# A fused attention-MLP-SSM kernel: the MLP's product a x GELU(g) moved from VectorE to ScalarE and GpSimd

## Chip, core and metric

One core of a Trainium2 chip, float32 throughout. The metric is the device time of one execution in microseconds; the time before is the median of three runs. The engines are TensorE (PE; its weight loads are shown apart as PEld), VectorE (DVE), ScalarE (ACT), GpSimd (POOL) and SyncE (SP), which here only starts DMAs.

## What is computed

x has 4096 tokens of 256. It is layer-normalized, two independent branches read the normalized tokens, and the output is x plus both. One branch is a Mamba block, the other a local transformer of two layers. Cut to what matters here, each transformer layer is:

```python
h = shift_token(x)                        # half of the channels come from the token before
q, k, v = split(h @ wqkv)                 # 8 heads of 64
q, k = rotary_xpos(l2norm(q) * qs, l2norm(k) * ks)
x = x + local_attention(q, k, v) @ wo     # windows of 128, each looks at itself and the one before
h = layernorm(shift_token(x)) * lg + lb   # over the 256 channels
a, g = split(h @ w1 + b1)                 # 682 columns each
x = x + (a * gelu(g)) @ w2 + b2           # gelu by erf
```

The Mamba block projects x to 512 channels and a gate, convolves over 4 tokens, and runs for each channel and each of 16 states the recurrence h = exp(dt*A)*h + dt*x*B over all tokens, sums h*C over the states, gates and projects back.

## The kernel before

**Tiling.** The transformer works in stages of 256 tokens: 2 layers x 16 stages = 32, each with two attention windows of 128. The Mamba block works in 8 blocks of 512 tokens, 4 groups of 128 channels, 16 states; two states are handled together, so `recur` runs 8 times for each block and channel group. In it GpSimd multiplies dt*x by the spread B (L793), ScalarE makes the decays exp(dt*A) in PSUM (L802), VectorE scans along the tokens (L807) and multiplies by the spread C (L817), ScalarE keeps the last column (L813), for some pairs GpSimd adds the two states (L825), and TensorE transposes and sums them into a PSUM bank y (L829). `bc` names the spread tiles, of which there are six.

**Projection and rotary (L905 to L995).** For each window TensorE makes q, k and v (L918, into PSUM banks `mm`). ScalarE squares and VectorE sums for the norms (L929, L931, L972). VectorE multiplies q by the two rotary tables (L963, L965), GpSimd adds the two products (L945). k is scaled by VectorE (L978), multiplied twice by GpSimd (L985), added by it (L945). TensorE transposes both (L950), ScalarE copies them out (L956). The products live in the buffer `turn`: five tiles, taken by two for q, one for the scaled k and two for its products. A work on q's matmuls holds its two tiles before it starts.

**Attention** scores, masks (L1032, a maximum goes to `top`), exponentiates (L1042), transposes (L1057), mixes (L1075) and projects out (L1116).

**The MLP stage (`mlp`, from L1134).** GpSimd adds the two halves of the channels (L1153), TensorE takes the mean, and so the layer norm proceeds to `hn` (L1171). The 682 columns of g and a are cut into five chunks of 128 and a last of 42. `up` (L1180) makes two chunks a time in one of five PSUM banks. `gates` does g: ScalarE evicts each chunk with its bias into `u` (L1196), the buffer `mlp` of one tile of 6 x 256 columns. The last chunk of g shares a matmul with the last chunk of a; ScalarE evicts that piece of a into `a5` (L1208). One ScalarE instruction takes GELU of all of `u` (L1217), between two loads of activation tables. GpSimd multiplies the last 42 rows by `a5` (L1222). `gated` then does the five other chunks of a: its matmuls wait for `u` after GELU, and VectorE adds the bias and multiplies by GELU(g) in one instruction for each chunk, from PSUM into `u` (L1230). `down` (L1243 in layer 0, L1262 in layer 1) multiplies by w2.

**Order.** The order isn't that of the program text. Each step is recorded by `add` with its engine, an estimated cost, what it reads and writes, and a lead `soon`. A step's key is its due time (`plan.key`, in stages; one stage of the transformer is 1.0) less `soon`. `Plan.order` simulates the engines with the estimated costs and buffers that come free, and gives each engine, when it is free, the ready step of the lowest key among those not over AHEAD beyond the earliest open one. So the leads and AHEAD fix each engine's queue; at run time the queues are in order and synchronized by semaphores. Buffers (L350 to L386) give tiles in the order of recording, the banks to whoever comes first. `port=True` marks VectorE steps that the planner keeps apart from GpSimd's.

The steps that the prediction speaks of also include: normalization of x (L579 to L606), the sum of x and attention, `mid` (L1122), the second in-projection products (L762 to L770), the finish (L546), and the Mamba output (L846 to L879).

Of the kernel before, what the change touches and what calls it, by code (L numbers as in the profile page):

```python
# [27 lines left out]
P = 128  # L28
# [14 lines left out]
AHEAD = 2.400000  # L43
# [275 lines left out]
def mamba_and_local_transformer(  # L319
# [27 lines left out]
    def buffer(name, n, shape, pool=work, any_first=False):  # L347
# [12 lines left out]
    turns = buffer("turn", 5, [P, HEADS, 2, DH // 2])  # L360
# [9 lines left out]
    lasts = buffer("a5", 1, [LAST, TS])  # L370
    small = {n: buffer(n, k, [P, w]) for n, k, w in (
        ("mv", 2, 2 * NW), ("rstd", 2, NW), ("nrm", 4, 2 * HEADS), ("top", 2, HEADS), ("den", 2, HEADS), ("mcol", 3, 1), ("tail", 2, CI * (TAPS - 1)),
# [82 lines left out]
    def load_small():  # L455
        dma(96, lambda: xpw.ap, lambda: xp_wT.rearrange("(c p) n -> p c n", p=P), writes=[xpw], soon=-0.27)
        for at_row in (0, DH):
            dma(32, lambda at_row=at_row: dtw.ap[at_row : at_row + DTR], lambda: dt_wT, writes=[(dtw, at_row)], soon=0.09)
        dma(128, lambda: b2row.ap, lambda: b2_d[DEPTH - 1 : DEPTH, :].partition_broadcast(P), writes=[b2row], soon=0.34)

    def load_qkv(l):
        for s in range(3):
            cut = slice(s * INNER, (s + 1) * INNER)
            dma(
                512, lambda cut=cut: wqkv.ap[:, :, cut],
                lambda cut=cut: wqkv_d[l][:, cut].rearrange("(k p) n -> p k n", p=P), writes=[(wqkv, s)], soon=-0.12,
            )

    def load_rest(l):
        dma(512, lambda: wo.ap, lambda: wo_d[l].rearrange("(h p) n -> p h n", p=P), writes=[wo], soon=-0.18)  # L470
        for half in range(2):
            for m, n in ((0, WHOLE), (NM - 1, LAST)):
                to, of = w1_at(half, m), half * HID + m * MC
                dma(
                    n, lambda to=to, n=n: w1.ap[:, :, to : to + n],
                    lambda of=of, n=n: w1_d[l][:, of : of + n].rearrange("(k p) n -> p k n", p=P),
                    writes=[(w1, (half, m))], soon=-1.18,
                )
# [3 lines left out]
            lambda: w2_d[l][0:whole, :].rearrange("(m p) n -> p m n", p=MC), writes=[(w2, 0)], soon=-1.27,  # L482
        )
        dma(42, lambda: w2.ap[0 : HID - whole, NM - 1, :], lambda: w2_d[l][whole:HID, :], writes=[(w2, 1)], soon=0.27)
# [28 lines left out]
        add("PE", 8.3, shift, [w1], [pb], soon=-0.56)  # L513
        add("DVE", 0.4, bias, [pb], [b1, b1x], soon=-1.5)
        add("DVE", 4.6, scale, [], [w1], port=True, soon=-0.19)
# [14 lines left out]
    def base_of(s):  # L530

        base = plan.value(rows_b)
        if s in sums:
            dma(256, lambda: base.ap, lambda: sums[s].ap, [sums[s]], [base], soon=-1.01)
            return base
        dma(256, lambda: base.ap, lambda: rows(x, s), writes=[base], soon=-0.2)
# [3 lines left out]
            ), [b2row], [base], soon=-1.46,  # L540
# [3 lines left out]
    def finish(s, po, base):  # L544

        add("DVE", 0.6, lambda: nc.vector.tensor_tensor(base.ap, halves(po), base.ap, ALU.add), [po], [base], soon=-1.31)  # L546
        if s in sums:
            dma(256, lambda: rows(out, s), lambda: base.ap, [base], soon=0.15)
            return
        sums[s] = plan.fixed(dram.tile([P, NW, D], F32, tag=f"sum{s}", name=f"sum{s}"))  # L550
        dma(256, lambda: sums[s].ap, lambda: base.ap, [base], [sums[s]], soon=0.04)
# [4 lines left out]
    def shift_column(l, s):  # L556
        now = xts[l, s]
        if s == 0:
            add("POOL", 0.14, lambda: nc.gpsimd.memset(now.ap[:, 1, 0:1], 0.0), [], [(now, 0)], soon=-0.23)
        else:  # L560
# [3 lines left out]
                [(old, 1)], [(now, 0)], soon=-0.63,  # L564
            )

    def normalize(s):
# [5 lines left out]
        dma(256, lambda: xb.ap, lambda: rows(x, s), writes=[xb], soon=0.01)  # L573
# [27 lines left out]
        add("DVE", 1.1, stats, [xb], [mv], soon=1.38)  # L601
        add("ACT", 0.5, root, [mv], [rstd], soon=0.58)
        add("DVE", 0.6, centre, [mv, rstd], [xb], port=True, soon=0.31)
        now = xts[0, s] = plan.value(tokens)
        add("PE", 0.44, turn, [xb], [pt], holds=[now], soon=0.21)
        add("ACT", 0.48, lambda: nc.scalar.copy(now.ap[:, :, 1:], halves(pt)), [pt], [(now, 1)], soon=0.22)  # L606
        shift_column(0, s)
        dma(256, lambda: xn_d[s].ap, lambda: now.ap[:, :, 1:], [(now, 1)], [xn_d[s]], soon=0.0)
# [3 lines left out]
    def reload(s):  # L612
        now = xts[1, s] = plan.value(tokens)
        dma(256, lambda: now.ap[:, :, 1:], lambda: x1_d[s].ap, [x1_d[s]], [(now, 1)], soon=-1.33)
# [6 lines left out]
    def in_half(i):  # L621
# [3 lines left out]
            lambda: in_wT[:, i * DI : (i + 1) * DI].rearrange("(k p) n -> p k n", p=P), writes=[w], soon=-0.73,  # L625
# [3 lines left out]
    def in_proj(b, w, c, to):  # L629
# [9 lines left out]
        add("PE", 1.72, emit, [w, xms[b]], [pm], holds=[to], soon=-0.05)  # L639
        return pm  # L640

    def front_load(b):
        xm = xms[b] = plan.value(xms_b)
        for i in range(PB):
            s = b * PB + i
            dma(
                256, lambda i=i: xm.ap[:, :, i * TS : (i + 1) * TS], lambda s=s: xn_d[s].ap, [xn_d[s]], [(xm, i)], soon=0.1
# [5 lines left out]
    def front_conv(b, c, w):  # L653
        xin, xc, tail = plan.value(rows_m), xcs[b], tails[b]
        edge = slice(c * (TAPS - 1), (c + 1) * (TAPS - 1))
        if b == 0:
            add("POOL", 0.14, lambda: nc.gpsimd.memset(xin.ap[:, 0 : TAPS - 1], 0.0), [], [(xin, 0)], soon=0.0)
        else:
# [3 lines left out]
                [(old, c)], [(xin, 0)], soon=-0.7,  # L662
            )
        pm = in_proj(b, w, c, xin)
        add("ACT", 0.48, lambda: nc.scalar.copy(xin.ap[:, TAPS - 1 :], pm.ap), [pm], [(xin, 1)], soon=0.34)
        if b < NB - 1:
            add(
                "POOL", 0.14, lambda: nc.gpsimd.tensor_copy(tail.ap[:, edge], xin.ap[:, TB:]), [(xin, 1)], [(tail, c)], soon=-0.09
            )
# [13 lines left out]
        for j in range(TAPS - 1):  # L683
            add("DVE", 0.7, lambda j=j: tap(j), [xin, pm], [(xc, c) if j == TAPS - 2 else pm], soon=1.05)

    def silu(v):
# [4 lines left out]
        add("ACT", 4.52, emit, [], [v], soon=0.03)  # L691

    def front_dbl(b):
# [3 lines left out]
        def emit():  # L697
# [9 lines left out]
        add("PE", 1.75, emit, [xc, xpw], [px], holds=[xd, part], soon=-0.05, part="columns")  # L707
        add("ACT", 0.48, lambda: nc.scalar.copy(part.ap[0:n, 0:TB], px.ap[DH : DH + n]), [px], [part], alone=[px], soon=-0.78)
        add(
            "DVE", 0.6, lambda: nc.vector.tensor_tensor(xd.ap[0:n], px.ap[0:n], part.ap[0:n, 0:TB], ALU.add),  # L710
            [px, part], [(xd, 0)], alone=[px], soon=0.43,
        )

        add("ACT", 0.48, lambda: nc.scalar.copy(xd.ap[DH : DH + DTR], xd.ap[0:DTR]), [(xd, 0)], [(xd, 1)], soon=-0.03)
        xds[b] = xd
        bc = bcs[b] = plan.fixed(dram.tile([2 * NS, TB], F32, tag=f"bc{b}", name=f"bc{b}"))
        dma(64, lambda: bc.ap, lambda: xd.ap[DTR:n, :], [(xd, 0)], [bc], soon=-1.47)

    def gate_conv(b, c, w):
# [4 lines left out]
        add("ACT", 0.48, lambda: nc.scalar.copy(sz.ap[:, c, :], pz.ap), [pz], [(sz, c)], soon=-1.3)  # L724

    def times(b, c):
# [12 lines left out]
        add("PE", 1.15, emit, [xd, dtw], banks2, holds=dts2, soon=0.34, part="rows")  # L739
        for i in range(2):  # L740
# [3 lines left out]
                ), [banks2[i]], [dts2[i]], soon=0.13,  # L744
# [3 lines left out]
    def prepare(b, c):  # L748

        if c % 2 == 0:  # L750
# [7 lines left out]
        add("ACT", 0.6, lambda: nc.scalar.activation(e.ap[:, n], dt.ap, AF.Abs), [dt], [e], soon=-0.9)  # L758
        add("ACT", 0.6, lambda: nc.scalar.activation(dt.ap, dt.ap, AF.Relu), [], [dt], soon=-1.46)
        add("ACT", 0.54, lambda: nc.scalar.activation(e.ap[:, n], e.ap[:, n], AF.Exp, scale=-1.0), [], [e], soon=0.57)  # L760
        add(
            "DVE", 0.36, lambda: nc.vector.tensor_scalar(r.ap[:, n], e.ap[:, n], 1.0, -1.0, ALU.add, ALU.add),  # L762
            [e], [r], port=True, soon=0.51,
        )
        add("POOL", 1.22, lambda: nc.gpsimd.tensor_tensor(r.ap[:, n], e.ap[:, n], r.ap[:, n], ALU.subtract), [e], [r], soon=-1.13)
        add("ACT", 0.6, lambda: nc.scalar.activation(e.ap[:, n], e.ap[:, n], AF.Ln, bias=one_t), [], [e], soon=0.18)
        add("POOL", 1.22, lambda: nc.gpsimd.tensor_tensor(dt.ap, dt.ap, r.ap[:, n], ALU.add), [r], [dt], soon=0.93)
        add("POOL", 1.22, lambda: nc.gpsimd.tensor_tensor(dt.ap, dt.ap, e.ap[:, n], ALU.add), [e], [dt], soon=-0.63)
        add(
            "DVE", 0.61, lambda: nc.vector.tensor_tensor(dtx.ap, dt.ap, xc.ap[:, c, :], ALU.mult),  # L770
            [dt, (xc, c)], [dtx], port=True, soon=-0.25,
# [3 lines left out]
    def recur(b, c, g):  # L775
# [6 lines left out]
        for s in range(2):  # L782
# [4 lines left out]
                .rearrange("n t -> (n t)").partition_broadcast(P), [bc], [w], soon=0.12,  # L787
# [7 lines left out]
            ), [dtx], [u], soon=-0.33,  # L795
        )
        for i in range(NG):
# [6 lines left out]
                ), [dt], [h], soon=0.69,  # L804
# [4 lines left out]
                ), [(u, i), (state, (c, n))], [h], soon=-1.12,  # L809
            )  # L810
            if b < NB - 1:
                add(
                    "ACT", 0.1, lambda h=h, n=n: nc.scalar.copy(state.ap[:, c, n : n + 1], h.ap[:, TB - 1 : TB]),  # L813
                    [h], [(state, (c, n))], alone=[h], soon=-0.07,
# [4 lines left out]
                ), [h, spread[1]], [(u, i)], alone=[h], soon=-0.23,  # L819
# [19 lines left out]
        for i in range(n_sums):  # L839
            add("PE", 0.44, lambda i=i: collect(i), [(u, i)], [y], soon=0.1)  # L840

    def close(b, c):
# [3 lines left out]
        add("ACT", 0.48, lambda: nc.scalar.copy(ytv(), y.ap), [y], [yt], soon=-0.11)  # L846

        def turn():
# [3 lines left out]
        add("PE", 0.44, turn, [yt], [py], soon=-0.54)  # L852
# [3 lines left out]
            ), [py], [(xc, c)], soon=-1.46,  # L856
# [3 lines left out]
            [sz], [(xc, c)], soon=-1.5,  # L860
        )

    def out_load():
# [3 lines left out]
            writes=[w], soon=-0.24,  # L867
# [3 lines left out]
    def out_proj(b, i, w):  # L871
# [12 lines left out]
        add("PE", 3.44, emit, [w, xc, base], [po], soon=-1.0)  # L884
# [5 lines left out]
    def rotation(l, s):  # L890
# [3 lines left out]
            writes=[rot], soon=-0.77,  # L894
        )
        for i, scales in enumerate((qks, qkw)):
            for q in range(2):
# [6 lines left out]
                    ), [rot], [(trig, (i, q))], soon=-0.27,  # L904
# [3 lines left out]
    def project(l, s, t):  # L908
# [19 lines left out]
        def norm(q, pm, sq):  # L928
            add("ACT", 0.48, lambda: nc.scalar.activation(sq.ap, pm.ap, AF.Square), [pm], [sq], alone=[pm], soon=0.5)  # L929
# [3 lines left out]
                ), [sq], [(nrm, q)], soon=-0.97,  # L933
# [10 lines left out]
        def turned(parts, to):  # L944
            add("POOL", 1.22, lambda: nc.gpsimd.tensor_tensor(parts[0].ap, parts[0].ap, parts[1].ap, ALU.add), [parts[1]], [parts[0]], soon=-0.57)  # L945
# [472 lines left out]
```

## Time and profile before

| what | value |
|---|---|
| runs | 1913.62, 1914.05, 1916.52 us; median 1914.05 |
| the profiled execution | 1914.12 us |
| its span, first to last instruction | 1912.3 us |
| mean granted TensorE clock | 0.992 of full |
| instructions | 37355 |
| DMA | 334.79 MB, mean 175 GB/s |

In the profile's groups, "out<-in" names tiles without buffer numbers, then partitions x elements and a count; after the bar stand busy us (overlap counted once), mean ns of one, and the engine's idle just before with what ended it. L numbers are lines of the kernel before. A row of waits is "engine output line <- who released it: us in total, times, longest". Matmul ends are modelled, so a busy TensorE isn't TensorE at its peak; a float32 matmul shows as two instructions.

### The profile page before, as it was taken

How to read it: one execution, taken by the hardware profiler on the slowest of the kernel's cores; microseconds unless marked ns; L12 is line 12 of the kernel's file. 1: busy time of each engine (PE TensorE's matmuls, PEld its weight loads, DVE VectorE, ACT ScalarE, POOL GpSimd, SP SyncE). 2: the span in 40 equal slices, each digit the busy share in tenths (PEclk: the TensorE clock that was granted, in tenths of full speed). 3: DMA queues.
4: the chain of work that ended last, by engine and by line, in shares of the span. 5: the costliest groups of instructions: out<-in, count | busy, mean ns of one | idle time of the engine just before them, and what ended most of it. 6: DMA issues, size and time to landing. Idle time of an engine off the chain costs nothing. (4 is left out here: it accounts for less than half of the span.)

```text
span 1912.3 us, 37355 instructions
## 1 busy us (share of the span) xinstructions
PE 1830.8 (96%) x13184; PEld 1359.3 (71%) x13184; DVE 1725.4 (90%) x3190; ACT 1543.8 (81%) x3634; POOL 1482.8 (78%) x1242
## 2 busy tenths in 40 slices
PE   7999999999999999999989999999999999999986
PEld 3676677776677767776767777777777777777775
DVE  5889899899999999898998799899999899899995
ACT  5887878879877788887977878797888798878673
POOL 3686787788877788877887678987888877887884
PEclk9999999999999999999999999999999999999999
DMA  5553555554555445565564555456455554544653
GB/s 171 177 169 131 171 169 166 183 177 150 174 188 197 157 137 183 173 205 183 190 210 167 180 196 174 161 201 206 133 175 182 183 185 166 183 171 164 200 177 140
DMA packets 133962, 334.79 MB, mean 175 GB/s; under 512 B 13468, under 2 KB 57200, under 8 KB 133776
## 3 DMA queue, kind: packets, MB, share of 16 engines
q1 hardware_dynamic: 133488, 332.21, 52.0%
q8 instruction: 104, 1.70, 0.4%
q14 instruction: 82, 0.67, 0.1%
q10 hardware_dynamic: 288, 0.20, 0.0%
HBM read 315.06 MB, written 17.30 MB: 174 GB/s over the span
## 5 line engine op out<-in xcount | busy, mean ns | idle before, releaser
L793 POOL TENSOR_TENSOR bc<-dtx,bc 128x1024 f32<-128x1024 f32 x256 | 606.0, 2368 | 190.9 <-DMA bc<-bc 146.0
L807 DVE TENSOR_TENSOR_SCAN da<-da,state,bc 128x512 f32<-128x512 f32 x448 | 564.6, 1279 | 52.3 <-ACT da L802 23.3
L802 ACT ACTIVATE da<-dt,negA 128x512 f32<-128x512 f32 x512 | 349.6, 694 | 81.1 <-DVE bc L817 76.4
L918 PE MATMUL mm<-wqkv,xt 128*128 128x512 f32 x768 | 362.2, 603 | 3.5 <-DVE turn L965 1.4
L817 DVE TENSOR_TENSOR bc<-da,bc 128x512 f32<-128x512 f32 x512 | 339.8, 678 | 7.7 <-ACT state L813 5.0
L1180 PE MATMUL mm<-hn,w 128*128 128x256 f32 (+1 forms) x1408 | 333.9, 384 | 7.7 <-DVE top L1032 4.2
L1180 PEld LDWEIGHTS mm<-hn,w 128*128 128x128 f32 (+1 forms) x1408 | 258.0, 189 | 67.2 <-issue 13.9
L825 POOL TENSOR_TENSOR bc<-bc 128x512 f32<-128x512 f32 x192 | 244.4, 1277 | 69.9 <-DVE bc L817 65.6
L1042 ACT ACTIVATE pr<-pr,top 128x256 f32<-128x256 f32 (+1 forms) x512 | 253.3, 500 | 18.2 <-DVE top L1032 17.9
L918 PEld LDWEIGHTS mm<-wqkv,xt 128*128 128x128 f32 x768 | 136.9, 192 | 129.4 <-issue 114.5
L1032 DVE CUSTOM_DVE_ANT_0 pr<-mm,maskf,nrm 128x256 f32<-128x256 f32 (+1 forms) x512 | 212.8, 472 | 6.3 <-PE mm L1017 3.3
L985 POOL TENSOR_TENSOR turn<-turn,trig 128x512 f32<-128x512 f32 x128 | 161.8, 1285 | 57.7 <-DVE turn L978 57.5
L829 PE MATMUL y<-ident,bc 128*128 128x128 f32 x1280 | 180.4, 277 | 19.8 <-POOL bc L825 19.6
L829 PEld LDWEIGHTS y<-ident,bc 128*128 128x128 f32 x1280 | 144.9, 141 | 54.7 <-POOL bc L825 27.6
L945 POOL TENSOR_TENSOR turn<-turn,turn 128x512 f32<-128x512 f32 x128 | 164.0, 1283 | 11.3 <-DVE turn L965 6.9
L1017 PEld LDWEIGHTS mm<-kT,qT 64*128 64x128 f32 x2016 | 125.7, 189 | 36.0 <-issue 12.4
L1017 PE MATMUL mm<-kT,qT 64*128 64x128 f32 x2016 | 145.1, 284 | 5.6 <-ACT kT L956 2.3
L1064 ACT COPY prT<-mm 128x512 f32<-128x512 f32 (+1 forms) x256 | 134.1, 581 | 13.4 <-PE mm L1057 12.5
L813 ACT COPY state<-da 128x1 f32<-128x1 f32 x448 | 70.9, 165 | 87.4 <-DVE da L807 71.5
L1075 PE MATMUL mm<-prT,v 128*64 128x128 f32 x2016 | 140.2, 281 | 0.5
L1075 PEld LDWEIGHTS mm<-prT,v 128*64 128x64 f32 x2016 | 113.9, 137 | 27.2 <-issue 8.0
L635 PE MATMUL mm<-xm,mw 128*128 128x512 f32 x256 | 123.2, 608 | 2.0 <-DVE xc L678 1.3
(132 smaller groups left out, 3370.5 us busy)
## 6 DMA issues: line engine op xcount, KB each, us to landing
bc<-bc SPq DMA_DIRECT2D x512, 512.0 KB, 4.6
io<-in_x SPq DMA_DIRECT2D x32, 256.0 KB, 4.9
mw<-in_in_wT SPq DMA_DIRECT2D x16, 512.0 KB, 5.3
rot<-in_rot SPq DMA_DIRECT2D x32, 128.0 KB, 2.2
xn<-xt SPq DMA_DIRECT2D x16, 256.0 KB, 2.8
xm<-xn SPq DMA_DIRECT2D x16, 256.0 KB, 4.3
x<-mid SPq DMA_DIRECT2D x16, 256.0 KB, 2.8
mw<-in_out_wT SPq DMA_DIRECT2D x8, 512.0 KB, 4.6
```

What stands on the lines that cost most here:

```text
L793: "POOL", 2.35, lambda: nc.gpsimd.tensor_tensor(u.ap, dtx.ap.unsqueeze(1).to_broadcast([P, NG, TB]), u.ap, ALU.mult), [dtx], [u], soon=-0.33,
L802: "ACT", 0.63, lambda h=h, n=n: nc.scalar.activation(h.ap, dt.ap, AF.Exp, scale=negA[:, c * NS + n : c * NS + n + 1]), [dt], [h], soon=0.69,
L807: "DVE", 1.18, lambda h=h, n=n, i=i: nc.vector.tensor_tensor_scan(h.ap, h.ap, u.ap[:, i, :], state.ap[:, c, n : n + 1] if b else 0.0, ALU. ...
L817: "DVE", 0.61, lambda h=h, i=i: nc.vector.tensor_tensor(u.ap[:, i, :], h.ap, spread[1].ap[:, i, :], ALU.mult), [h, spread[1]], [(u, i)], a ...
L825: add("POOL", 1.22, lambda: nc.gpsimd.tensor_tensor(u.ap[:, 0, :], u.ap[:, 0, :], u.ap[:, 1, :], ALU.add), [], [u], soon=-1.5)
L829: nc.tensor.matmul(y.ap[:, t, :], lhsT=u.ap[:, i, t * P : (t + 1) * P], rhs=ident, is_transpose=True, start=g == 0 and i == 0 and t == 0, ...
L918: nc.tensor.matmul(pm.ap, lhsT=hT[k], rhs=wqkv.ap[:, k, q * INNER : (q + 1) * INNER], start=k == 0, stop=k == KC - 1,)
L1017: nc.tensor.matmul(halves(scs[j])[:, i, a * WIN : (a + 1) * WIN], lhsT=qT.ap[half, 2 * g + i, :], rhs=kk.ap[half, 2 * g + i, :], start=n == 0,
L1032: nc.vector.tensor_tensor_reduce(out=prs[j].ap[:, i, keys], in0=halves(scs[j])[:, i, keys], in1=mask[:, keys], scale=nrm.ap[:, h : h + 1], ...
L1042: nc.scalar.activation(prs[j].ap[:, i, keys], prs[j].ap[:, i, keys], AF.Exp, bias=top.ap[:, h : h + 1], scale=-1.0, accum_out=den.ap[:, h ...
L1075: nc.tensor.matmul(hpair(po.ap)[j * DH : (j + 1) * DH, hp, :], lhsT=vv.ap[:, h * DH : (h + 1) * DH], rhs=prT.ap[:, i, j, a, :], start=a == ...
L1180: nc.tensor.matmul(halves(pm)[0:r, i, :], lhsT=w1.ap[:, k, c0 : c0 + r], rhs=hn.ap[:, k, :], start=k == 0, stop=k == KC - 1,)
```

## The change

In the MLP, ScalarE evicts each chunk of a with its bias into a new buffer `ga` of two tiles of 2 x 256 columns, and GpSimd multiplies `u` by it: chunks 0 and 1 in one instruction, 2 and 3 in one, chunk 4 alone, and the last 42 rows as before. The matmuls of a no longer wait for `u`. The tile `a5` becomes the second half of one `ga` tile; chunk 4 takes its first half. `turn` goes from five tiles to four, and the small buffer `nrm` from four to three. AHEAD goes from 2.4 to 2.84, and nearly all of the leads `soon` in the kernel have new values. Instructions elsewhere, and their shapes, are the same.

```diff
-AHEAD = 2.400000
+AHEAD = 2.84
...
-    turns = buffer("turn", 5, [P, HEADS, 2, DH // 2])
+    turns = buffer("turn", 4, [P, HEADS, 2, DH // 2])
...
-    lasts = buffer("a5", 1, [LAST, TS])
+    gains = buffer("ga", 2, [P, 2, TS])
...
-        ("mv", 2, 2 * NW), ("rstd", 2, NW), ("nrm", 4, 2 * HEADS), ("top", 2, HEADS), ("den", 2, HEADS), ("mcol", 3, 1), ("tail", 2, CI * (TAPS - 1)),
+        ("mv", 2, 2 * NW), ("rstd", 2, NW), ("nrm", 3, 2 * HEADS), ("top", 2, HEADS), ("den", 2, HEADS), ("mcol", 3, 1), ("tail", 2, CI * (TAPS - 1)),
...
-        def up(tiles, after=()):
+        def up(tiles):
...
-            add("PE", 0.86 * len(tiles), emit, [hn, w1, *after], [pm], soon=0.11)
+            add("PE", 0.86 * len(tiles), emit, [hn, w1], [pm], soon=0.21)
...
-        add("ACT", 4.1, gelu, [], [u], soon=-1.05)
-        add(
-            "POOL", 0.68, lambda: nc.gpsimd.tensor_tensor(u.ap[0:LAST, last, :], u.ap[0:LAST, last, :], a5.ap, ALU.mult),
-            [a5], [(u, last)], soon=-0.03,
-        )
-
-        def gated(ms):
-            pm = up([(w1_at(0, m), MC) for m in ms], [u])
+        add("ACT", 4.1, gelu, [], [u], soon=-1.42)
+
+        def times_gain(a, m, n, rows=P):
+            at = m % 2
+            add(
+                "POOL", 0.68 if n == 1 else 1.22, lambda: nc.gpsimd.tensor_tensor(
+                    u.ap[0:rows, m : m + n, :], u.ap[0:rows, m : m + n, :], a.ap[0:rows, at : at + n, :], ALU.mult
+                ), [(a, m) if n == 1 else a], [(u, m + i) for i in range(n)], soon=-0.83,
+            )
+
+        times_gain(a45, last, 1, LAST)
+
+        def gated(ms, a):
+
+            pm = up([(w1_at(0, m), MC) for m in ms])
             for i, m in enumerate(ms):
                 add(
-                    "DVE", 0.39, lambda i=i, m=m: nc.vector.scalar_tensor_tensor(
-                        u.ap[:, m, :], halves(pm)[:, i, :], b1.ap[:, 0, m : m + 1], u.ap[:, m, :], ALU.add, ALU.mult
-                    ), [pm, b1], [(u, m)], soon=-0.63,
+                    "ACT", 0.38, lambda i=i, m=m: nc.scalar.activation(
+                        a.ap[:, i, :], halves(pm)[:, i, :], AF.Identity, bias=b1.ap[:, 0, m : m + 1]
+                    ), [pm, b1], [(a, m)], soon=-0.95,
                 )
+            times_gain(a, ms[0], len(ms))
 
         for ms in ((0, 1), (2, 3), (4,)):
-            gated(ms)
+            gated(ms, a45 if len(ms) == 1 else plan.value(gains))
```

Some of the leads that change most, elsewhere (before, after): the loads of wqkv -0.12, 0.43; of x1 back for layer 1 -1.33, 0.97; the spread of B and C 0.12, -0.56; the k products L985 1.5, 0.24; the norm sums L931 -0.97, 0.0; down in layer 0 -0.3, 0.63, in layer 1 -0.92, 1.16; the mix of attention 0.48, 0.0.

## Prediction

> **What bounds the kernel now.** I read the page's busy shares and slices first, then the busy table of chosen stretches, then TensorE's waits and the other engines' waits, and last the groups by form. The page's lines:
>
> ```profile
> PE 1830.8 (96%) x13184; PEld 1359.3 (71%) x13184; DVE 1725.4 (90%) x3190; ACT 1543.8 (81%) x3634; POOL 1482.8 (78%) x1242
> PE   7999999999999999999989999999999999999986
> ```
>
> TensorE is the bound: 1912.3 - 1830.8 = 81.5 us of idle is all that a better order can win without touching its matmuls. VectorE, at 90%, comes next. The table of stretches (columns: stretch, length, busy us of PE, PEld, DVE, ACT, POOL with instruction counts, clock, DMA share, GB/s) says where the idle lies:
>
> ```profile
> 0.00:50.00 50.00, 38.75 (x147) 18.98 (x148) 26.67 (x70) 29.59 (x67) 18.92 (x49) 0.97 0.56 177
> 950.00:1000.00 50.00, 44.95 (x304) 33.01 (x304) 46.26 (x82) 39.69 (x103) 44.61 (x35) 1.00 0.60 201
> 1100.00:1150.00 50.00, 50.00 (x378) 36.09 (x377) 48.56 (x93) 39.26 (x92) 36.74 (x33) 1.00 0.55 186
> 1850.00:1900.00 50.00, 34.58 (x194) 29.03 (x193) 39.62 (x50) 21.01 (x32) 30.92 (x20) 0.93 0.50 174
> 1900.00:1912.30 12.30, 7.53 (x36) 6.00 (x34) 2.13 (x3) 0.00 (x0) 1.26 (x1) 0.93 0.19 64
> ```
>
> The start holds 11.3 us of it, the last 62 us hold 15.4 + 4.8 = 20.2, the middle 1800 us the other 50. Between 1100 and 1150 TensorE never rests; between 950 and 1000 it rests 5 us, where GpSimd is at its busiest. TensorE's waits, then two of GpSimd's from the waits of all engines (us in total, times, longest):
>
> ```profile
> PE y L829 <- POOL bc L825: 19.6, 16, 6.5
> PE mm L950 <- POOL turn L945: 9.6, 9, 3.0
> PE mm L597 <- DVE io L589: 7.2, 1, 7.2
> PE mm L1180 <- DVE top L1032: 4.2, 5, 1.3
> ```
>
> ```profile
> POOL bc L793 <- DMA bc<-bc: 146.0, 84, 7.8
> POOL bc L825 <- DVE bc L817: 65.6, 40, 5.0
> ```
>
> By direct releaser, the listed TensorE waits sum to 33 us for GpSimd, 25.6 for VectorE (7.2 of it the start's) and 14.4 for ScalarE. But GpSimd's L825, which releases the largest, itself waits 65.6 us for VectorE's L817: the root of that row is VectorE. The rows that cost the change:
>
> ```profile
> L817 DVE TENSOR_TENSOR bc<-da,bc 128x512 f32<-128x512 f32 x512 | 339.8, 678 | 7.7 <-ACT state L813 5.0 <-DMA bc<-bc 0.3
> L1230 DVE SCALAR_TENSOR_TENSOR mlp<-mm,b,mlp 128x256 f32<-128x256 f32 x160 | 71.0, 471 | 4.9 <-PE mm L1180 4.8
> L1196 ACT ACTIVATE mlp<-mm,b 128x256 f32<-128x256 f32 x160 | 68.4, 469 | 22.2 <-PE mm L1180 21.2
> L825 POOL TENSOR_TENSOR bc<-bc 128x512 f32<-128x512 f32 x192 | 244.4, 1277 | 69.9 <-DVE bc L817 65.6 <-DVE nrm L972 2.4 <-DMA bc<-bc 2.0
> L1161 POOL TENSOR_TENSOR sq<-sq 128x256 f32<-128x256 f32 x32 | 23.5, 733 | 8.1 <-ACT sq L1159 6.4 <-ACT state L813 1.8
> ```
>
> **What leaves VectorE.** The 160 fused L1230 instructions (5 in each of 32 MLP stages) go: 71.0 us busy, or 2.2 us a stage of 1912.3/32 = 59.8 us. VectorE falls to 1654.4 us, 86.5% of the same span; its idle rises from 187 to 258 us.
>
> **What ScalarE gets.** 160 evictions with a bias, 128x256 from a PSUM bank: exactly L1196's form, so 68.4 us. ScalarE rises to 1612.2 us, 84.3%. Each is queued in order; behind it wait the decays L802 and the exponentials L1042, and whoever waits for those waits up to two evictions (0.84 us) longer.
>
> **What GpSimd gets.** In each stage two products of 128x512 and one of 128x256. L825 and L1161 are the same operation and shapes: 64 x 1.277 + 32 x 0.733 = 81.7 + 23.5 = 105.2 us; the 42-row product stays. GpSimd rises to 1588 us, 83.0%. Behind each product in its queue stand L793 (the input of the scans), L825 (for which TensorE's y waits) and L945 (before the q and k transposes).
>
> **The rule against it.** The Trainium skill ("GPSIMD Engine Reference", 3. Performance versus the Vector engine) advises keeping ordinary elementwise work on VectorE, about twice as fast. The rows agree on the speed (1277 against 678 ns for 128x512), and the sum of engine time gets worse: 71.0 out, 68.4 + 105.2 = 173.6 in. By the rule the change loses, by up to the extra 102.6 us if GpSimd or ScalarE set the end. I weigh it against the page: after the change the four engines stand at 96, 86, 84 and 83%, so no engine but TensorE can be the bound by load. The order, not the sum, decides.
>
> **The port.** The skill's "SBUF — State Buffer" (Who interferes with whom) says that a VectorE instruction with at most one SBUF input, outside the two-port modes, doesn't contend with GpSimd, while two-port ones and GpSimd lock each other out for a whole instruction. L1230 has one SBUF tensor and one from PSUM: it contended with nothing. The new products do. The trace shows such a loser, I infer (columns: count, then ns least/median/most):
>
> ```profile
> L972 DVE TENSOR_SCALAR nrm<-nrm x64: 154/165/2329, 16.0 to 1824.2; 128x16 f32<-128x16 f32 x64
> ```
>
> Its mean is 429 ns by the groups, so (429 - 165) x 64 = 17 us are lost there. With GpSimd's share up by 5.5 points of 77.5 that grows by 1.2 us; full blocking by every added product of half a product's length at each of the 224 port-using instructions (L972, L1092, L589, L770, L762) would be at most 224 x 0.64 x 0.055 = 8 us. I take 1.
>
> **The GELU wait.** The matmuls of a waited for the whole GELU; now only the products do. TensorE's idle before L1180 is 7.7 us in all, none of it released by GELU, so the gain is 0 and at most 1 us. What hides it is the list of other works that the planner puts between; `hidden` has one buffer, but its stage (L1196 at 1869.9 to the last down matmul at 1896.8 in the last stage) covers 27 of 59.8 us, so three products after GELU don't make it the bound.
>
> **One rotary tile less, one norm tile less.** With four tiles, kparts' second takes the place of a q tile, free once q is transposed; the next window's q matmuls hold two tiles and can now start only after both L985 of this one. Below: nothing, since GpSimd's 57.5 us before L985 wait for VectorE, not tiles. Above: 64 windows x one half L985 (0.64) = 41 us, if TensorE had nothing else; the nearest row is its 3.5 us of idle before L918. I take 3.
>
> **The leads and AHEAD.** No instruction comes from them, but every queue is rearranged, SP's loads with it. No row prices it. Below: the middle's 50 us regained; above: 5 us lost in each 50, as in 950 to 1000, over 1800, some 180. Near the first rather: most stretches lie within 1 us of full. I take -6, an estimate.
>
> **The sum.** Waits rooted in VectorE in the middle: L829's 19.6 less the 13.0 that the timeline has in the last 62 us, L950's 9.6, and VectorE's own 25.6 - 7.2 = 18.4; together 34.6 us. If a wait goes as busy over idle (a rule of thumb, my choice), VectorE's ratio falls from 9.2 to 6.4, by 30%: -10.4 us. ScalarE's rises from 4.2 to 5.4, by 28% of 14.4: +4.0. GpSimd's rises by 42%; of its own waits only 33 - 29.2 = 3.8 us aren't counted above: +1.6. At the tail L1230 lies on the chain of waits between 1884 and 1891 (its five instructions, 2.2 us), where GpSimd has room: -2.2. Port +1, tile +3, leads -6, GELU 0. Sum -9.0; this on the profiled execution's 1914.12 us (span 1912.3 and 1.8 around it, 0.07 above the runs' median) is 1905. What isn't in the idle is the delay within busy stretches, too short for the profile to call it a wait; it should move the same way, and I add half of the sum without tile and leads (-6.0), that is -3. That gives 1902. 0.2% (3.8 us) is about what a measurement can tell here.
>
> **Rivals.** (1) GpSimd's queue becomes the one waited for: slower. A wide product set ahead of L825 or L793 puts 1.28 us before a scan or a y transpose. It decides from the point where such delays exceed the 12 us saved: when more than 9 of the 96 products, a tenth, each hold TensorE for their length. For it: 950 to 1000, GpSimd at 44.6, TensorE idle 5 us; 33 us of direct waits. Against: its 190.9 us idle before L793 is room, if the products fall there. If a quarter of the 105.2 us comes through to TensorE, +26 - 12 = +14: 1928. (2) The missing tile bites: q matmuls late by 0.4 us in each of 64 windows, +26 in place of the 3 in a sum of -12, so +11: 1925. Against: TensorE's small idle before L918. (3) VectorE was not the root; its waits just change names (L825 waits for the DMA behind L793, 146 us today): 1914.
>
> **Numbers.** Forecast (faster: 1902, its own range 1878 to 1910) 0.53; rival 3, no change, 0.10; rival 1 0.26; rival 2 0.11. So faster 0.53, within 0.2% 0.10, slower 0.37; the range runs from 1878 (45% of the 81.5 us of idle gone, with the leads at their best) to 1940 (rival 1 with 36% of the 105.2 us seen by TensorE: +38 - 12).
>
> **What would show it.** VectorE near 1654 us, ScalarE near 1612, GpSimd near 1588 show the costs. TensorE's wait at L829 for L825 below 19.6 us, and the middle's idle below 50, show the forecast. Rival 1: more TensorE and scan (L807) waits released by GpSimd, with products just before them. Rival 2: idle before the projection matmuls above 3.5 us. Most likely to prove me wrong: the rearranged order, which no row of this trace bears on.

## The result and the profile after

The changed kernel takes 1931.96 us (median of 6 runs, 1927.09 to 1942.15), the kernel before beside it 1915.28 us: a ratio of 1.0091, 95% interval [1.0063, 1.012]. It is slower by 17 us, where 12 us of gain were forecast. The profiled execution is one of 1927.09 us. One of the four executions of run 3 below took 9547 us, in the chip's slow state, and is left out there.

The page after, busy time by engine and TensorE's slices:

```profile
span 1925.3 us, 37429 instructions
PE 1836.9 (95%) x13184; PEld 1368.2 (71%) x13184; DVE 1706.7 (89%) x3030; ACT 1597.7 (83%) x3794; POOL 1582.8 (82%) x1338
PE   7999999999999999999999999999999999999996
```

ScalarE rose by 53.9 us and GpSimd by 100.0, near what was worked out. VectorE did not fall by 71.0 us but by 18.7. Some 52 us of the relief are missing, and the groups of VectorE show where they are. (Lines up to L1171 have the same numbers in both kernels; L1195, L1225 and L1237 are the g eviction, GpSimd's products and the a eviction.)

```profile
L972 DVE TENSOR_SCALAR nrm<-nrm 128x16 f32<-128x16 f32 x64 | 50.1, 782 | 0.2
L770 DVE TENSOR_TENSOR dtx<-dt,xc 128x512 f32<-128x512 f32 x32 | 43.0, 1342 | 3.8 <-POOL dt L768 2.9 <-POOL bc L793 0.8
L589 DVE TENSOR_SCALAR io<-io,mv,rstd 128x256 f32<-128x256 f32 x32 | 30.6, 999 | 3.2 <-ACT rstd L585 2.1 <-PE mm L950 1.0
L762 DVE TENSOR_SCALAR m2k<-m2k 128x512 f32<-128x512 f32 x32 | 19.6, 614 | 0.5 <-ACT m2k L760 0.4
```

The same groups before:

```profile
L972 DVE TENSOR_SCALAR nrm<-nrm 128x16 f32<-128x16 f32 x64 | 27.5, 429 | 0.2
L589 DVE TENSOR_SCALAR io<-io,mv,rstd 128x256 f32<-128x256 f32 x32 | 26.9, 884 | 0.9 <-ACT rstd L585 0.9
L770 DVE TENSOR_TENSOR dtx<-dt,xc 128x512 f32<-128x512 f32 x32 | 25.1, 783 | 0.6 <-POOL bc L793 0.6
L762 DVE TENSOR_SCALAR m2k<-m2k 128x512 f32<-128x512 f32 x32 | 17.7, 552 | 0.0
```

Four instructions that the change does not touch became longer. The least, median and most of a single one (the last three numbers after the count) say that it isn't their work; the last row is L770 before:

```profile
L972 DVE TENSOR_SCALAR nrm<-nrm x64: 154/297/3158, 14.9 to 1846.3; 128x16 f32<-128x16 f32 x64
L770 DVE TENSOR_TENSOR dtx<-dt,xc x32: 667/687/4308, 68.9 to 1857.1; 128x512 f32<-128x512 f32 x32
L770 DVE TENSOR_TENSOR dtx<-dt,xc x32: 669/681/1784, 60.7 to 1850.2; 128x512 f32<-128x512 f32 x32
```

The shortest are as short as before (154 ns for L972, in the prediction's row, and 669 for L770); the longest take over 3 and 4 us. I call the time above the shortest form, (mean - least) x count, an instruction's excess. Before it was 17.6 us for L972, 3.6 for L770, 16.8 for L589 (least 358) and 4.6 for L762 (least 409), together 42.6; after it is 40.2, 21.6, 20.5 (least 359) and 6.5 (least 410), together 88.8. The growth is 46.2 us, most of the missing relief of 52 (busy time counts overlapping instructions once, so the two sums need not agree). The timeline at one long L972 (start, length, engine, instruction) shows what it lasts for:

```profile
517.51 1.95 POOL L1225 TENSOR_TENSOR mlp<-mlp,ga 128x512 f32<-128x512 f32 x2
...
518.64 3.16 DVE L972 TENSOR_SCALAR nrm<-nrm 128x16 f32<-128x16 f32 x1
...
519.43 2.33 POOL L793 TENSOR_TENSOR bc<-dtx,bc 128x1024 f32<-128x1024 f32 x1
521.71 1.28 DVE L807 TENSOR_TENSOR_SCAN da<-da,state,bc 128x512 f32<-128x512 f32 x1
521.83 0.22 ACT L938 ACTIVATE nrm<-nrm 128x16 f32<-128x16 f32 x1 [2.37 <-DVE nrm L972]
...
522.29 0.57 ACT L991 COPY v<-mm 128x512 f32<-128x512 f32 x1
...
522.91 0.47 PE L597 MATMUL mm<-ident,io 128*128 128x128 f32 x1 [2.99 <-ACT v L991]
```

A clip of 16 columns starts while two of the new products run, sits through their end and the whole of L793 that follows without a gap, and is done at 521.80, when GpSimd is (519.43 + 2.33 = 521.76). An engine that waits inside an instruction is counted as busy: no list of waits names these 89 us. Behind the clip a scan and ScalarE's logarithm (idle 2.37 us) stand still, behind the logarithm in ScalarE's queue a copy (L991), and behind the copy TensorE (idle 2.99 us).

The example stands for the rest. Call long what takes over 0.1 us more than the shortest of its group: before, 46 of the 160 instructions of the four groups are long, after, 72. Each of the 72 ends a nearly fixed time after a GpSimd instruction ends: L972 27 to 34 ns, L589 146 to 153, L762 281 to 285, L770 546 to 591. Of the 46, one lasts over more than one GpSimd instruction; of the 72, 18 do, over two to four that follow without a gap.

TensorE's waits, for those that the prediction shows of before, and the scans' wait for L793, after and then before:

```profile
PE y L829 <- POOL bc L825: 4.9, 7, 1.5
PE mm L950 <- POOL turn L945: 6.0, 12, 1.4
PE mm L597 <- DVE io L589: 7.6, 2, 7.4
...
DVE da L807 <- POOL bc L793: 38.0, 22, 4.3
DVE da L807 <- POOL bc L793: 15.0, 15, 2.5
```

The waits that the forecast wanted smaller are smaller (19.6 to 4.9 and 9.6 to 6.0 us), but TensorE's idle is 1925.3 - 1836.9 = 88.4 us in place of 81.5: other waits took their place. Between the start's 50 us and the last 62 it idles for 62.8 us, where the forecast wanted less than 50.

That is 6.9 us of the 13.0 between the two profiled spans. The other 6.1 us are longer TensorE busy time, and the granted clock bears on them. Two stretches around the long clip show it (columns as in the prediction: length, busy us of PE, PEld, DVE, ACT and POOL, then the clock):

```profile
519.90:522.50 2.60, 0.02 (x2) 0.00 (x0) 2.60 (x2) 0.64 (x3) 1.86 (x1) 1.00 0.00 0
522.50:529.30 6.80, 6.39 (x41) 5.46 (x42) 6.52 (x21) 6.40 (x22) 5.56 (x7) 0.50 0.24 78
```

TensorE stands still, and then works for 6.8 us at half its clock. (A matmul of L918 takes 1061 ns in this trace's half-clock stretches and 592 outside, by the medians.) In this trace the clock is halved in 11 stretches, 51.1 us together; before, in 7, 32.4 us. Half of that is lost, 25.6 against 16.2 us: up to 9.4 us of the 13.0. Eight of the 11 stretches begin during a standstill of TensorE or within 1.2 us of its end, but six standstills of over 1.5 us are followed by none, so no rule comes out of this.

### The profile page after: what moved, and what is told of

Read it like the earlier page. It is cut to its first block, busy times and chain, and to the rows that moved or that the text cites. A ratio compares the mean times of both kernels' runs of the same rounds, so it can differ in the third digit from the quotient of the medians.

```text
span 1925.3 us, 37429 instructions
## 1 busy us (share of the span) xinstructions
PE 1836.9 (95%) x13184; PEld 1368.2 (71%) x13184; DVE 1706.7 (89%) x3030; ACT 1597.7 (83%) x3794; POOL 1582.8 (82%) x1338
## 5 line engine op out<-in xcount | busy, mean ns | idle before, releaser
L793 POOL TENSOR_TENSOR bc<-dtx,bc 128x1024 f32<-128x1024 f32 x256 | 605.6, 2368 | 131.3 <-DMA bc<-bc 105.1
L918 PE MATMUL mm<-wqkv,xt 128*128 128x512 f32 x768 | 366.9, 606 | 7.3 <-DVE xc L678 2.7
L1180 PE MATMUL mm<-hn,w 128*128 128x256 f32 (+1 forms) x1408 | 316.1, 382 | 3.1 <-DVE hn L1171 2.5
L1180 PEld LDWEIGHTS mm<-hn,w 128*128 128x128 f32 (+1 forms) x1408 | 263.4, 190 | 47.4 <-DVE hn L1171 4.7
L918 PEld LDWEIGHTS mm<-wqkv,xt 128*128 128x128 f32 x768 | 136.6, 193 | 131.9 <-issue 112.1
L985 POOL TENSOR_TENSOR turn<-turn,trig 128x512 f32<-128x512 f32 x128 | 161.6, 1283 | 55.7 <-DVE turn L978 41.0
L1225 POOL TENSOR_TENSOR mlp<-mlp,ga 128x512 f32<-128x512 f32 (+2 forms) x128 | 126.4, 1003 | 12.5 <-ACT ga L1237 7.9
```

Of the source, the lines that this page charges most:

```text
L793: "POOL", 2.35, lambda: nc.gpsimd.tensor_tensor(u.ap, dtx.ap.unsqueeze(1).to_broadcast([P, NG, TB]), u.ap, ALU.mult), [dtx], [u], soon=-0.26,
L918: nc.tensor.matmul(pm.ap, lhsT=hT[k], rhs=wqkv.ap[:, k, q * INNER : (q + 1) * INNER], start=k == 0, stop=k == KC - 1,)
L1180: nc.tensor.matmul(halves(pm)[0:r, i, :], lhsT=w1.ap[:, k, c0 : c0 + r], rhs=hn.ap[:, k, :], start=k == 0, stop=k == KC - 1,)
```

## The experiments

Theory A: VectorE's instructions that take two SBUF inputs (L770), or that are a tensor-scalar in SBUF (L972, L589, L762), wait for GpSimd's running row of instructions, and the new products made those rows longer. Rivals: B, GpSimd's own load and queue delay the scans and TensorE; C, the new leads are the loss; and the missing tile. Every ratio is to the kernel before, run beside it. Edits marked "order kept" change only what a step emits; the planner's order is the same. The edits are cut to the part that counts. Where a factor, a clip or a product is left out, or tiles are too few, the output is not the reference's, and the run is for its time alone.

**1 and 2. The waits taken away, order kept.** In each kernel both lines become sums over one element, with one input; the clip and the factor x are left out:

```diff
-lambda: nc.vector.tensor_scalar_max(nrm.ap, nrm.ap, NORM_MIN**2)
+lambda: nc.vector.tensor_reduce(nrm.ap, nrm.ap.unsqueeze(2), AX.X, ALU.add)
-lambda: nc.vector.tensor_tensor(dtx.ap, dt.ap, xc.ap[:, c, :], ALU.mult)
+lambda: nc.vector.tensor_reduce(dtx.ap, dt.ap.unsqueeze(2), AX.X, ALU.add)
```

> The changed kernel with its planned order; the clip of the norms (L972) and the product dt*x (L770) are replaced by sums over one element on VectorE, which read one SBUF tile: the clip and the factor x are left out. Theory A (VectorE's instructions that need the port shared with GpSimd wait longer, since GpSimd runs back to back: in excess of their shortest forms they hold 89 us in the profile after, 44 in the one before): L972 falls from 782 to about 165 ns and L770 from 1342 to about 680, VectorE's busy time by some 60 us, and the kernel by 15 to 25 us, to 1907 to 1917. Theory B (GpSimd's queue itself makes the scans and TensorE late, whoever holds the port): VectorE's busy time falls as well, but the kernel by less than 8 us, so 1924 or more.

> The same edit on the kernel before; the clip and the factor x are left out. Theory A: only some 21 us of VectorE's time go, so the kernel falls by 4 to 9 us, to 1906 to 1911, and the distance between the two kernels closes to 6 us or less from the 17 of the medians. Theory B: the distance stays at 12 us or more.

The changed kernel fell to 1898.84 us, 0.9931 [0.9906, 0.9956]; the kernel before to 1906.62, 0.9967 [0.9952, 0.9981]. Relative to their own times that is 1.6% (31 us) against 0.3% (6 us). More than expected of A, and the sign turned: without these waits the change is a gain of 0.9931/0.9967 = 0.4%. The groups of the changed kernel without them:

```profile
L770 DVE TENSOR_REDUCE dtx<-dt 128x512 f32<-128x512 f32 x32 | 21.6, 676 | 3.7 <-POOL dt L768 2.9 <-POOL bc L793 0.8
L972 DVE TENSOR_REDUCE nrm<-nrm 128x16 f32<-128x16 f32 x64 | 10.3, 162 | 0.2
```

The sums take 668 to 686 and 150 to 171 ns, although 22 of the 32 and 39 of the 64 run beside a GpSimd instruction (for over 0.1 us). The scans still wait 45.1 us for L793 in this kernel of 1899 us, so that wait isn't what made the change slow.

**3. No wide products, order kept.** The 96 new products are not issued; ScalarE still evicts.

```diff
-nc.gpsimd.tensor_tensor(
+rows < P and nc.gpsimd.tensor_tensor(
```

> The changed kernel with its planned order, without the 96 wide products on GpSimd (the product of a and GELU(g) is left out for all but the last 42 columns); the evictions stay. Theory A: GpSimd back near 1478 us busy, L972 and L770 nearer their lengths before, the kernel falls by 20 to 30 us to 1902 to 1912, of which most is what the removal of the lock alone gives. Theory B: it falls by as much or more, to 1890 to 1905, and by at least 15 us more than the removal of the lock alone. If the evictions on ScalarE or the order were the cost: less than 8 us, 1924 or more.

1895.5 us, 0.9912 [0.9887, 0.9937]: below theory A's range and inside B's. But taking the products away, 99 us of GpSimd's time, won only 4 us more than taking the waits alone, within the intervals: theory B's further 15 us aren't there. The excess of L972 and L770 fell to (503 - 157) x 64 + (852 - 668) x 32 = 22 + 6 = 28 us from 61.8: the products cause about 34 us of it; the 7 us by which it stays above the 21.2 of before are the new order's. The scans wait 40.6 us for L793 here too, so that wait comes with the order, not with the products. Of the waits of the four groups, 66 are still long here, but only 2 reach over more than one GpSimd instruction: the order makes more instructions wait, the products make the waits longer.

**4. The relief alone, order kept.** The kernel before without its fused instructions:

```diff
-nc.vector.scalar_tensor_tensor(u.ap[:, m, :], halves(pm)[:, i, :], b1.ap[:, 0, m : m + 1], u.ap[:, m, :], ALU.add, ALU.mult)
+None
```

> The kernel before with its planned order, without the 160 fused instructions of VectorE (bias and product of the first 640 columns are left out). It prices what the change could win at best. The prediction's step (34.6 us of TensorE's waits rooted in VectorE, 30% of them gone, 2.2 at the tail): 8 to 16 us, 1899 to 1907. If VectorE isn't the root: within 4 us of 1915.

1902.74 us, 0.9948 [0.9928, 0.9969]: 10 us, in the forecast's range. Taking VectorE's fused instructions away, with nothing given to anyone, buys no more than this. (VectorE's busy time fell by 48.9 us: part of the 71 overlapped with neighbours, and the waits of L972 grew, from a mean of 429 to 554 ns.)

**5 and 6. The clip without VectorE, order kept.** The constant of the clip is added in the logarithm instead; the whole reference is computed.

```diff
-nc.scalar.activation(nrm.ap, nrm.ap, AF.Ln, scale=65536.0)
+nc.scalar.activation(nrm.ap, nrm.ap, AF.Ln, scale=65536.0, bias=tiny_t)
-lambda: nc.vector.tensor_scalar_max(nrm.ap, nrm.ap, NORM_MIN**2)
+lambda: None
```

> The changed kernel with its planned order; the clip L972 on VectorE is gone, and its constant goes into the logarithm's bias on ScalarE, so that the whole reference is computed. Theory A (the lock is the cause): L972's 50 us of VectorE go, 40 of them waits for the port; of the 33 us that went with both L972's and L770's waits (61 us together) about two thirds, so 1932 - 20 = 1912, within 1905 to 1918. Theory B (only L770, on the way from dt to the scans, counts; L972 has cover): less than 8 us, 1924 or more.

> The same edit on the kernel before. L972's 27.5 us go, 17 of them waits. Theory A: most of the 6 us that went with both edits, so 1907 to 1911. Theory B: 1911 to 1914.

1912.45 us, 0.9999 [0.9983, 1.0015], and 1908.84 us, 0.9975 [0.996, 0.999]. In the changed kernel this won 0.9% of the 1.6%, as A expected. The four groups' excess is 51.6 us here and 52.6 in run 3, yet run 3 is faster by 0.9%. Either the waits that are left count for less there, or the products cost something of their own as well; no run takes away both the products and the waits.

**7 and 8. dt*x on GpSimd, order kept.** In the changed kernel L770's `nc.vector.tensor_tensor` becomes `nc.gpsimd.tensor_tensor`; alone, and then together with edit 5.

> The changed kernel with its planned order, but the product dt*x (L770) is done by GpSimd at the same place in the order; the whole reference is computed. VectorE loses 43 us, of which 21 are waits for the port; GpSimd gains 32 x 1.28 = 41 us. Theory A: GpSimd's own load matters less than the lock, so it gains 5 to 15 us, 1917 to 1927. Theory B (L770's waits count since it stands before the scans): 15 us or more, 1917 or less. If GpSimd's load is the cost: no gain or a loss, 1932 or more.

1948.8 us, 1.0187 [1.0133, 1.0242]: a miss for theory A. The group of L972 says why:

```profile
L972 DVE TENSOR_SCALAR nrm<-nrm 128x16 f32<-128x16 f32 x64 | 88.1, 1376 | 0.3
```

It grew from 782 to 1376 ns, 38 us: 21 of its 64 now last over two to five GpSimd instructions, where 10 lasted over two or three; VectorE's busy time stayed at 1707.4 us although 43 us of L770 had left it. That could be the whole loss, or GpSimd's load could be, and the next run parts the two.

> The changed kernel in its planned order, with both of the two edits that keep the reference whole: no clip on VectorE (its constant in the logarithm's bias) and dt*x on GpSimd. Alone, the second edit made it slower (1.019 of before), and in its profile L972 grew from 50 to 88 us: L770's wait for the port had moved to L972. Theory A (the port): with L972 gone there is nothing for it to move to but L589 and L762, VectorE's busy time falls below 1640 us, and the kernel comes to 0.99 to 1.000 of before. Theory B (GpSimd's load and its queue made that run slow): it stays above 1.005 although VectorE's waits are gone.

1898.82 us, 0.9915 [0.9897, 0.9933], as A expected:

```profile
PE 1823.7 (96%) x13184; PEld 1358.6 (72%) x13184; DVE 1631.7 (86%) x2934; ACT 1599.8 (84%) x3794; POOL 1617.3 (85%) x1371
```

GpSimd carries as much as in run 7 (1617.3 against 1618.8 us), the scans wait 49.9 us for L793, and the kernel is 2.7% faster than with the clip. Load on GpSimd wasn't what made run 7 slow; an instruction of VectorE that waits for it was. This version computes the whole reference and beats both kernels. The kernel before with the same two edits was not run, so this doesn't compare the structures.

**9. The leads alone.** The kernel before with the new leads and AHEAD.

> The kernel before (fused product on VectorE, five rotary tiles, four norm tiles) with the changed kernel's leads and AHEAD. Theory C (the leads are the loss, whatever the products do): 1930 or more, as slow as the changed kernel, and it would have to keep VectorE's lock waits near 44 us. Theory A (the leads aren't the loss by themselves, but they were fitted to the other structure): between 1915 and 1950, with lock waits of L972 and L770 near 21 to 28 us, so that the loss, if any, has another source. This run tells of the leads only in this structure.

1983.55 us, 1.0367 [1.0333, 1.0402]: beyond theory A's 1950, and in theory C's range of time, but without the waits of 44 us that C asked for: the excess of L972 and L770 is (535 - 154) x 64 + (895 - 660) x 32 = 32 us. In the structure of before these leads cost 71 us. The run says nothing on whether they are good in their own.

**10. The tiles alone, order kept.** Four real rotary tiles and three norm tiles under the order of before.

```diff
-return self.buffer.tiles[self.slot]
+return self.buffer.tiles[self.turn % n if n else self.slot]   # n = 4 for turn, 3 for nrm
```

> The kernel before, its planned order kept, with only four real tiles for the rotary products and three for the norms; the plan's fifth tile is in use in 0.5% of the order's steps, so in a few windows products are overwritten too early and the output of those is changed. Rival 2 of the prediction (the missing tile makes the projection late): 8 us or more slower than before. Theory A (the tiles aren't the loss): within 3 us of before, with TensorE's idle before L918 near 3.5 us.

1912.79 us, 1.0004 [0.999, 1.0018]. The tiles cost nothing at this order.

**11. The MLP alone in the order before.** Each fused step emits an eviction, each second one a product; tiles as in run 10.

```diff
-nc.vector.scalar_tensor_tensor(u..., halves(pm)[:, i, :], bias, u..., ALU.add, ALU.mult)
+nc.scalar.activation(ga[:, i, :], halves(pm)[:, i, :], AF.Identity, bias=bias)
+if i == len(ms) - 1: nc.gpsimd.tensor_tensor(u[pair], u[pair], ga[pair], ALU.mult)
```

> The change of the MLP alone in the order before: at each place of a fused VectorE instruction ScalarE evicts, and after the second of a pair GpSimd multiplies; four rotary and three norm tiles as in the run before; leads and AHEAD as before. Theory A (GpSimd's products lengthen VectorE's waits for the port whatever the leads): excess of L972, L589, L770 and L762 above 60 us in place of 41, VectorE's busy time falls by less than 50 us, the kernel stays within 12 us of before on either side. Theory C (the leads after are what lengthens the waits): the excess stays near 41 us, VectorE falls by 65 us or more, and the kernel gains 5 us or more. Theory B (GpSimd's queue delays the scans): slower by 10 us or more with more waiting of L807 for L793.

1991.45 us, 1.0415 [1.0382, 1.0449]: far slower than A or C expected, so inconclusive between them. The excess of the four lines is 72 us, so the products lengthen the waits at the old leads as well. Theory B's signs are there too: the scans wait 22.8 us for their input in place of 15.0. The loss has a source that is small in the changed kernel (7.9 us there):

```profile
POOL mlp L1241 <- ACT ga L1239: 40.8, 28, 4.5
```

L1241 is here the product, L1239 the eviction. At the place of the fused instruction the product is at the head of GpSimd's queue before its operand is there. The change needed leads of its own.

**12 to 15. Leads found anew for both structures.** Both without the clip, in the code and in the plan, their leads searched by the planner's own end to within 1.5 us of each other; then each with the one-input sum for dt*x, order kept.

> The changed kernel without the clip L972 (its constant in the logarithm's bias; the whole reference is computed), the step taken out of the plan as well, and leads searched again for it by the planner's own end, which is as early as that of the changed kernel. Theory A (what the lock took is what was lost): as the changed kernel without the clip or better, 1895 to 1914. Theory C (what counts is how an order turns out on the chip, and one that the planner likes is as likely bad): above 1920.

> The same with the fused product on VectorE and the tiles of before: no clip, leads searched again to a planner's end equal to the other's within 1.5 us. Theory A with the relief worth what the runs without locks gave (7 us between the kernels): 4 to 10 us slower than the other run, about 1902 to 1918. If the relief of VectorE is worth nothing once the leads are fitted: within 3 us of the other, or faster.

1922.87 us, 1.004 [1.0017, 1.0062], and 1897.76 us, 0.9912 [0.9886, 0.9939]: theory A's first expectations failed, the changed structure came out where theory C put it (above 1920), and the structure of before won by 1.3%. L770 (here L772) shows why; the changed structure stands first:

```profile
L772 DVE TENSOR_TENSOR dtx<-dt,xc 128x512 f32<-128x512 f32 x32 | 51.2, 1601 | 0.0
```

```profile
L772 DVE TENSOR_TENSOR dtx<-dt,xc 128x512 f32<-128x512 f32 x32 | 25.3, 790 | 1.1 <-POOL bc L795 1.0
```

> The run with new leads and the products on GpSimd, its order kept, but L770's product dt*x is a sum over one element that reads one SBUF tile; the factor x is left out. L770's excess is 29.5 us there. Theory A (the port): it falls by 10 us or more from 1.004 of before, to 0.999 or less, and comes within 8 us of its counterpart below. Theory B (GpSimd's own load or the order): less than 5 us, and 12 us or more remain between the two.

> The same edit with new leads and the fused product on VectorE; the factor x is left out. L770's excess is 3.7 us there: both theories expect 0 to 4 us less than 0.991 of before.

Without it: 1901.33 us, 0.9934 [0.9916, 0.9952], against 1902.96 us, 0.9947 [0.9928, 0.9967]. The distance of 1.3% is gone in a second pair of orders, by the same edit. Some 1.1% of it is what the changed structure won. The rest is that the structure of before became 0.35% slower, where up to 4 us of gain were expected; the intervals of its two ratios overlap, and the cause is open.

## Why the prediction was wrong, step by step

- **What leaves VectorE**: the 71.0 us left. As relief they are worth 10 us at the order before (run 4), the size of the steps "-10.4" and "-2.2" together. With the half added for short delays those would be 19, for which the run gives no sign.
- **What ScalarE and GpSimd get**: 53.9 us for 68.4 (the eviction's group has 71.2 us busy; other groups give the rest back or overlap), and 100.0 for 105.2. Right.
- **The port** is the step that failed: "full blocking ... would be at most ... 8 us. I take 1". VectorE's excess grew by 46.2 us, and the kernel lost 31 - 6 = 25 us more to these waits than the kernel before did, so this term alone holds most of the 29 us between forecast and result. The sum had counted only L972's 17 us of waits, of 42.6 that the four groups already had, and let them grow with GpSimd's busy share. Its bound took a wait as half of one product, 0.64 us. The row quoted there, 2329 ns at most, was already longer: a wait lasts to the end of the GpSimd instruction that runs, L793 with its 2.37 us among them, and on over those that follow without a gap. Both the number of long ones (46 to 72) and the excess for each (0.9 to 1.2 us on average) grew. The Trainium skill ("SBUF — State Buffer", Who interferes with whom) says that whoever issues first gets the pair for its whole instruction, while the other blocks; the runs agree on who waits, but 18 of the 72 waits reach over two to four of GpSimd's instructions.
- **The rule against the change**: weighed down because no engine but TensorE could be the bound by load. That holds: run 8 has GpSimd at 1617.3 us and is faster than the kernel before. The price of work on GpSimd was, for the most part, in VectorE's row, not in GpSimd's.
- **Rival 1** had the sign, not the mechanism: the scans' wait for L793 rose from 15.0 to 38.0 us, but is 40.6 without the products and 45.1 in the kernel of 1899 us. That its 1928 us lies near the 1932 measured is luck, as far as the runs show.
- **Rival 2**, and the step "I take 3": the tiles cost 0 within 0.2% at the order before. TensorE's idle before L918 did rise, from 3.5 to 7.3 us, with the new order; L678, L956 and L1237 released most of it, none of them a reader of `turn`. What the fourth tile costs inside the new order no run shows.
- **The leads**, "-6": can't be read from one run alone. They cost 4% in the structure of before. In their own, with the waits gone, the change gives 0.4% (first orders) and 0.1% (leads searched anew, within the intervals' width).
- **Rival 3** (VectorE not the root) is answered by run 4: it was, for 10 us.

Why the planner accepted such leads can be read in the code, though no run tests it: a step with `port=True` starts at `max(start, port["POOL"])`, the end of the one GpSimd step that runs. The further steps of the row are not charged. Not settled is why a wait can reach over several GpSimd instructions, whether by arbitration or by what is already queued; no run here looks into it. It is also inferred, not shown, that the shared thing is a port: what is shown is that the waits end with GpSimd's instructions, and that one-input sums in the same places don't wait.

## What to carry to other kernels

Before work is moved to GpSimd, list the instructions of VectorE whose longest is many times their shortest: each is a place where VectorE can stand still inside an instruction, and the sum can grow far faster than GpSimd's share (here from 43 to 89 us as that went from 78 to 82%). Take those instructions away first: into a bias, as in run 5, or to GpSimd itself, as in run 8. Take them together, since a wait taken from one can move to the next (run 7). And compare two structures only with orders fitted to each, or with the order kept.

## What the runs showed of the hardware

- A tensor-scalar of 128x16 takes 154 ns and up to 5643 (L972 in run 7); the one-input sum of the same tile takes 150 to 171 ns in the same order (run 1).
- The reciprocal L1092 has the same place in the plan's list of port steps, but never waits: 168 to 204 ns before, 169 to 204 after, where 34 of its 64 run beside a GpSimd instruction.
- The mean granted TensorE clock was 0.987 after and 0.992 before in the profiled executions. It goes with the time: executions of the kernel before alone (those beside runs 5 to 7 and 9) range from 1904.49 us at 0.993 to 1919.73 at 0.987. So part of the loss of 17 us is paid through the clock. It isn't a cause apart from the waits as far as the runs show: with the waits taken away in the same order (run 1) it was 0.988 to 0.992, against 0.981 to 0.988 in the changed kernel. No run holds the clock fixed.
